# A second Strassen level for one product of seven, and what comes with it, in a four-layer graph-attention stack in fp32

## The chip, the cores and the metric

The kernel runs on one core of a Trainium2 chip. The metric is the device time of one execution in microseconds. Everything is fp32.

## The reference

The input `x` is 128 graphs of 64 nodes of 512 features, 8192 rows in all; `adj` is one 64 x 64 mask for all of them. Four layers follow one another, each `x = x + f(relu(layernorm(x)), adj)`:

```
layer 0: q, k, v = h@W + b;  softmax(q k^T / 8 + mask) v         8 heads of 64, no output product
layer 1: the same, then @ Wo + bo
layer 2: q = h Wq^T, k = h Wk^T, v = h Wv^T
         rel = adj^T * (q k^T);  rel / norm(rel, rows);  rel v   one head of 512
layer 3: qkv = h @ w_qkv;  masked softmax, as above;  o = (...) @ w_proj + b_proj
         f = o + layernorm(o) * gamma + beta
```

## The kernel before

**Tiling.** The rows are cut into 16 blocks of 512 tokens (`NB` = 16, `T` = 512), eight graphs each; a step `n` of the main loop is one block of one layer, 64 steps in all. A block's activations lie in SBUF as `hT`, features on partitions, so that TensorE can contract over them. Layer 2's q and k are folded into one matrix `a2` = Wq^T Wk ahead of time, so it has two projections (`g` and `v`); layer 0 has three (q, k, v), layers 1 and 3 four (q, k, v, o).

**Projections by Strassen.** A projection is a 512 x 512 by 512 x 512 product. It is done by Strassen's method with seven products of 256 x 256 by 256 x 256 in place of eight (`projection`, with `prod_T` for transposed and `prod_N` for plain results). The sums on the activations' side are `sums_x` (into `S` for `hT`, into `SO` for the attention's output `oT`, on POOL), those on the weights' side `sums_w`. Each of the seven products is four matmuls 256 columns wide into one PSUM bank. `ORDER` says in which order they run; two products that are added up share a bank (`X`). After each, ACT or DVE takes the bank out: product 1 to `s1`, 6 and 7 plus `s1` to `u2` and `u3`, 5 to `z5`, and the four corners Y11 (product 2), Y12 (3), Y21 (4, plus `u3`) and Y22 (`u3` + `z5`, on POOL) go where the `emit_...` function in use says.

**Attention.** `attend` runs in pieces between the projections: scores on TensorE (64 x 64 tiles, four at a time), mask and row maximum on DVE, subtraction on POOL, exponential on ACT, sum on DVE, scaling on POOL, and a transpose. `turn` is that transpose, used for `hT` too: DVE splits the fp32 words into two planes of 16 bits (`z`), SP issues a DMA transpose into `hp`, ACT joins the planes again. Then the products with v follow (`finish0` in layer 0, `finish13` in layers 1 and 3).

**Residual.** `load_xo` loads the block's input into `xo`; POOL adds a row of biases to it in layers 0, 1 and 3. In layer 3, `tail3` does the second layernorm: statistics of `o` on DVE, `xo += o` on POOL in four pieces, and two DVE instructions for each of the four tiles, the second one into `xo`. The tile `o` lies in `kT`'s buffer.

**Order of work.** All instructions are first recorded in `Plan`, in the order of the program, with the data that they read and write. `Plan.order` then schedules them as a list: for each engine, the ready step with the lowest rank comes next, by costs and latencies from `duration`; steps that read PSUM are moved up by `RUSH`. The result is a fixed order for each engine, issued as it stands. All instructions therefore carry the line of `record`, L193, in the profile, and are told apart by their tiles. Between the products of a projection, `tick` lets the waiting pieces of work (layernorm, attention, loads) record their next part.

**Buffers.** PSUM has eight banks: a ring of four for projections (`ps_mm`) and two double banks for attention (`ps_so`). In SBUF, `z` is a ring of four, `hp` of three, `s` (scores) of four, `xo` of two, and `qT`, `kT`, `v`, `oT`, `SO` are single.

```
ORDER = (1, 6, 5, 2, 7, 3, 4)
X = {1: 1, 2: 1, 6: 6, 7: 6, 5: 5, 3: 5, 4: 4}
```

Of the kernel before, what the change touches and what calls it, by code (L numbers as in the profile page):

```python
# [43 lines left out]
ORDER = (1, 6, 5, 2, 7, 3, 4)  # L44
ORDER0 = (1, 2, 5, 6, 3, 7, 4)
# [10 lines left out]
class Plan:  # L56
# [4 lines left out]
    def __init__(self, nc):  # L61
        self.nc = nc
        self.steps, self.products = [], []
        self.wrote, self.readers, self.known = {}, {}, {}
        self.group = None
        for e in ("tensor", "vector", "scalar", "gpsimd", "sync"):
            setattr(self, e, Engine(self, e))
# [48 lines left out]
    def add(self, eng, calls, reads, writes, busy, late):  # L116
# [12 lines left out]
        self.steps.append((eng, calls, deps, busy, late))  # L129

    def order(self):
        n = len(self.steps)
        wait = [len(s[2]) for s in self.steps]
        users = [[] for _ in range(n)]
        for i, s in enumerate(self.steps):
            for d in s[2]:
                users[d].append(i)

        rank = [i - RUSH * any(v.tensor.name.startswith("mm_") for c in s[1] for v in c[1][1:] if isinstance(v, bass.AP)) for i, s in enumerate(self.steps)]
# [10 lines left out]
        while len(out) < n:  # L150
# [17 lines left out]
            eng, _, _, busy, late = self.steps[i]  # L168
            if e == "sync":
                moved = max(moved, at + 1400) + late / 180  # L170
                late = moved + 600 - at - busy
            elif e == "vector" and late == PORT:
                busy += max(0.0, free["gpsimd"] - at)
                port = at + busy
            elif e == "gpsimd":
                busy += max(0.0, port - at)
            free[e] = at + busy
            out.append((at, i))
            for u in users[i]:
                same = self.steps[u][0] == e  # L180
                ready[u] = max(ready[u], at + busy + (0.0 if same and e != "sync" else late))
# [36 lines left out]

PORT = 150.5
RUSH = 60  # L220
# [4 lines left out]
def duration(eng, op, aps, a, k):  # L225
# [3 lines left out]
    if eng == "tensor":  # L229
# [3 lines left out]
        pass_ = max(n, P if m > HD else HD) * 0.842  # L233
# [17 lines left out]
    if eng == "gpsimd":  # L251
        if n <= HD:
            return (1010 if ALU.pow in a else 310), 120
        return n * (1.82 if n > D else 2.41), 120
    size = (2 if out.dtype == U16 else 4) * n * out.partition_size()
    return 1270 if k.get("transpose") else 520, size
# [3 lines left out]
def gnn_stack_kernel(  # L260
# [17 lines left out]
    def pool(name, bufs, **kw):  # L278
        return Ring(ctx.enter_context(tc.tile_pool(name=name, bufs=1, **kw)), bufs)

    const, wp, p1, p2, p4, p8, p3 = (
        pool("const", 1), pool("w", 4), pool("p1", 1), pool("p2", 2), pool("p4", 4), pool("p8", 8), pool("p3", 3),
    )
    rows = pool("rows", 3)
    sm = pool("sm", 4)
    dram = ctx.enter_context(tc.tile_pool(name="dram", bufs=1, space=bass.MemoryType.DRAM))
    ps_mm = pool("ps_mm", 4, space=bass.MemoryType.PSUM)
    ps_so = pool("ps_so", 2, space=bass.MemoryType.PSUM)
# [10 lines left out]
    pw = ps_mm.tile([P, KC, P], F32, tag="mm", name="pw")  # L299
# [3 lines left out]
    def dma(dst, src):  # L303
        plan.sync.dma_start(dst, src)

# [36 lines left out]
    def load_w(name, src):  # L342

        w = wp.tile([P, 7, 2, H2], F32, tag="w", name=name)


        def part(i, j):
            return src[i * H2 : (i + 1) * H2, j * H2 : (j + 1) * H2].rearrange("(c p) f -> p c f", p=P)

        dma(w[:, W11], part(0, 0))  # L350
        dma(w[:, W21], part(1, 0))
        dma(w[:, WT3], part(0, 1))
        dma(w[:, W22], part(1, 1))
        return w

    def sums_w(w, eng):
        tt = eng.tensor_tensor
        tt(w[:, WT1], w[:, WT3], w[:, W11], ALU.subtract)
        tt(w[:, WT2], w[:, W22], w[:, WT1], ALU.subtract)
        yield 1  # L360
# [3 lines left out]
    W = {}  # L364

    def weight(name, src, eng=gps):
        W[name] = load_w(name, src)
        yield 4
        yield from sums_w(W[name], eng)

# [4 lines left out]
    first = [load_w("q0", wq0)]  # L375
# [4 lines left out]
    first += [load_w("k0", wk0)]  # L380
# [16 lines left out]
    def raw(tag, src, nm):  # L397
        t = p1.tile([P, KC, D], F32, tag=tag, name=nm)
        for c in range(KC):
            dma(t[:, c, :], src[c * P : (c + 1) * P, :])  # L400
            yield 3
        return t

    def fold():
# [4 lines left out]
        for dc in range(KC):  # L409
            pa = ps_mm.tile([P, D], F32, tag="mm", name=f"pfa_{dc}")  # L410
# [4 lines left out]
            f = p4.tile([P, D], F32, tag="z", name=f"fa_{dc}")  # L415
            act.copy(f, pa)
            yield 1
# [4 lines left out]
        for ec in range(KC):  # L422
            f = p4.tile([P, KC, P], F32, tag="z", name=f"ft_{ec}")
            turn(f, rv[:, ec, :], f"v2_{ec}")
            yield 1
            dma(v2d.rearrange("(c p) e -> p c e", p=P)[:, :, ts(ec, P)], f)
            yield 1
# [17 lines left out]
    hTs, Ss, vs = {}, {}, {}  # L445
    ready = set()

    def turn(dst, src, nm):


        zp = p4.tile([P, D], F32, tag="z", name=f"zp_{nm}").bitcast(U16).rearrange("p (w f) -> p w f", w=2)
        dve.tensor_copy(zp, src.bitcast(U16).rearrange("p (f w) -> p w f", w=2))
        hp = p3.tile([P, 2, KC, P], U16, tag="hp", name=f"hp_{nm}")
# [5 lines left out]
    def layer_norm(n):  # L459
# [19 lines left out]
        if n == 0:  # L479
            for t in range(NT):  # L480
                z = xins[n][t]
                act.activation(z, z, AF.Relu, bias=nb[:, t : t + 1], scale=rs[:, t : t + 1])
                pt = ps_mm.tile([P, KC, P], F32, tag="mm", name=f"pz_{n}_{t}")
# [4 lines left out]
                if t == 1:  # L488
                    for i in range(WARM // 2):
                        pe.transpose(pw[:, i % KC, :], xins[n][0][:, ts(i % KC, P)], ident)  # L490
                (dve.tensor_copy if t else act.copy)(hT[:, :, ts(t, P)], pt)
        for t in range(NT) if n else ():
# [8 lines left out]
    def sums_x(tag, src, nm, eng):  # L501
# [7 lines left out]
        return {1: x11, 2: x12, 3: S[:, 3], 4: x22, 5: S[:, 0], 6: S[:, 1], 7: S[:, 2]}  # L509
# [19 lines left out]

    def projection(prod, w, xop, nm, emit, order=ORDER):  # L530

# [3 lines left out]
        def bank(i):  # L535
            banks[i] = ps_mm.tile([P, D], F32, tag="mm", name=f"pp{i}_{nm}")
# [6 lines left out]
        X = {1: 1, 2: 1, 6: 6, 7: 6, 5: 5, 3: 5, 4: 4}  # L543
        for i in order:
# [4 lines left out]
            prod(ps, w[:, BLOCKS[i]], xop()[i], first)  # L549
# [16 lines left out]
            elif i == 3:  # L566
                emit("Y12", ps, tmp["u2"])
            if i != order[-1]:
# [4 lines left out]
    def emit_plain(region):  # L573

        def emit(what, a, b=None):
# [15 lines left out]
    def emit_bias(region, bias):  # L591

        def emit(what, a, b=None):
# [37 lines left out]
    def scores(qT, kT, g, nm):  # L631

        pss = ps_so.tile([P, 2, 2, KC, G], F32, tag="so", name=f"pss_{nm}")
        for p in range(2):
            for c in range(KC):
                for h, x in QUARTERS:
                    b = h ^ x
                    at = ts(4 * g + 2 * p + b, G)  # L640
                    pe.matmul(
                        pss[half(x), b, p, c, :], qT[half(h), c, at], kT[half(h), c, at], start=True, stop=True
                    )
        return pss

    def attend(n, qT, kT, v, done):

        l = n // NB
        plan.begin()
        psss = [scores(qT, kT, g, f"{n}_{g}") for g in range(2)]  # L650
        plan.end(300)
        ss = [p4.tile([P, 2 * KC, 2, G], F32, tag="s", name=f"s_{n}_{g}") for g in range(2)]
        yield 1
        for s, pss in zip(ss, psss):
            for b in range(2):
                dve.tensor_tensor(
                    s[:, :, b, :], pss[:, b].rearrange("p q c j -> p (q c) j"),
                    MASKS[l].unsqueeze(1).to_broadcast([P, 2 * KC, G]), ALU.add,
                )
            sf = s.rearrange("p q b j -> p (q b) j")  # L660
# [3 lines left out]
            yield 2  # L664
        yield 1
        for s in ss:
# [6 lines left out]
            yield 2  # L673
        yield 1

        aTs = []
        for s in ss:
            aT = s.rearrange("p (q c) b j -> p q c (b j)", q=2)
            aTs.append(aT)
            for p in range(2):  # L680
                if n < N - 1:
                    turn(aT[:, p], s[:, p * KC : (p + 1) * KC].rearrange("p c b j -> p (c b j)"), f"a_{n}_{p}")
                else:
                    pt = ps_mm.tile([P, KC, P], F32, tag="mm", name=f"pa_{n}_{p}")
# [4 lines left out]
                    act.copy(aT[:, p], pt)  # L689
                yield 1  # L690
        yield 1
        yield from done(aTs, v)
# [25 lines left out]
    def load_xo(n):  # L718
# [5 lines left out]
        if l in xo_row:  # L724
            row = R[xo_row[l]]
            for t in range(NT):
                gps.tensor_tensor(xos[n][:, t, :], xos[n][:, t, :], row, ALU.add)
                if t < NT - 1:
                    yield 1
        ready.add(("xo", n))  # L730

    def finish0(n):
        def done(aTs, v):


            assert ("xo", n) in ready and ("v", n) in ready
            plan.begin()
            pos = []
            for g, aT in enumerate(aTs):
                po = ps_so.tile([P, 2, 2, H2], F32, tag="so", name=f"po_{n}_{g}")  # L740
                pos.append(po)
                for p in range(2):
                    for c2 in range(2):
                        for h in range(2):
                            for b, y in QUARTERS:
                                j = b ^ y
                                f = c2 * P + h * HD
                                pe.matmul(
                                    po[half(y), j, p, f : f + HD], aT[half(b), p, 2 * j + c2, half(h ^ b)],
                                    v[half(b), 2 * g + p, j * H2 + f : j * H2 + f + HD], start=True, stop=True,  # L750
                                )
            plan.end(300)
            yield 1
            for g, po in enumerate(pos):
                for j in range(2):
                    xv = xos[n][:, 2 * g : 2 * g + 2, j * H2 : (j + 1) * H2]
                    dve.tensor_tensor(xv, po[:, j], xv, ALU.add)
            yield 1
            store(n, xos[n])
        return done  # L760
# [3 lines left out]
    def finish13(n):  # L764
        def done(aTs, v):

            assert ("v", n) in ready
            oTs[n] = p1.tile([P, KC, T], F32, tag="oT", name=f"oT_{n}")
            plan.begin()
            pos = []  # L770
            for g, aT in enumerate(aTs):
                po = ps_so.tile([P, 2, 2, KC, G], F32, tag="so", name=f"po_{n}_{g}")
                pos.append(po)
                for p in range(2):
                    for c in range(KC):
                        for b, h in QUARTERS:
                            f = c * P + h * HD
# [347 lines left out]
```

## Time and profile before

| What | us |
|---|---|
| median of 3 runs | 2843.88 (2843.86 to 2844.54) |
| the profiled execution, its own time | 2844.57 |
| its span, first to last instruction | 2842.8 |
| TensorE busy | 2828.4 |
| VectorE (DVE) busy | 2037.6 |
| GpSimd (POOL) busy | 1840.5 |
| ScalarE (ACT) busy | 1248.0 |

PE stands for TensorE's matmuls and PEld for its weight loads, which run beside them. Granted clock of TensorE in the profiled execution: 0.999. A group of instructions reads as engine, operation, result<-operands by tile names, shape, count, then busy time in us, mean ns of one, and the idle time ahead of them with what ended it. Busy time of matmuls counts overlapping records once; a record is longer than the distance to the next. SP issues all DMAs; the 16 DMA engines were busy for half of the span (50.0%).

### The profile page before, as it was taken

Reading aid. Unit: us, or ns where it says so; the run is one execution under the profiler, and the core shown is the slowest. Engines: PE = TensorE matmul, PEld = TensorE weight load, DVE = VectorE, ACT = ScalarE, POOL = GpSimd, SP = SyncE. Lnnn points to the kernel's source line nnn. Section 1 sums busy time; section 2 is a strip of 40 time slices with the busy share of each in tenths; the row PEclk is TensorE's granted clock in tenths of the full one; section 3 lists DMA queues with packets and bytes.
Section 4 is the critical chain, followed back from the end, with each engine's and each line's share of the span. In section 5 each row is a group of like instructions: output and inputs, shape, how many; then the busy total and the mean of one; then the engine's idle time right before and its main releaser. Section 6 shows DMA issues by size and latency. Waiting matters only on the chain.

```text
span 2842.8 us, 62036 instructions
## 1 busy us (share of the span) xinstructions
PE 2828.4 (99%) x25833; PEld 2471.6 (87%) x25833; DVE 2037.6 (72%) x3104; ACT 1248.0 (44%) x1589; POOL 1840.5 (65%) x1349
## 2 busy tenths in 40 slices
PE   9999999999999999999999999999999999999998
PEld 8878888888888888888888888888888888888887
DVE  7767778876767767667666555555688888778787
ACT  4555555454443534534434343443444444444442
POOL 6555566656766667667677334344678687787796
PEclk9999999999999999999999999999999999999999
DMA  6766666556453533533546565756433433433432
GB/s 158 163 137 156 143 146 134 127 128 163 105 120 80 124 95 82 131 85 86 136 114 156 136 162 143 164 128 157 120 86 94 119 86 95 112 91 96 109 84 66
DMA packets 634890, 342.29 MB, mean 120 GB/s; under 512 B 485232, under 2 KB 566384, under 8 KB 634608
## 3 DMA queue, kind: packets, MB, share of 16 engines
q1 hardware_dynamic: 634608, 338.32, 50.0%
q8 instruction: 202, 3.31, 0.5%
q14 instruction: 80, 0.66, 0.1%
HBM read 152.61 MB, written 69.21 MB: 78 GB/s over the span
## 4 chain that ended last, share of the span: by engine, by line
PE 96%; DVE 3%; issue 0%; POOL 0%; DMA 0%; ACT 0%; POOLq 0%; SPq 0%; DVEq 0%
PE mm L193 88%; PE so L193 8%; DVE z L193 1%; DVE st L193 0%; POOL s L193 0%; DVE u L193 0%; DVE sr L193 0%; DVE kT L193 0%; DMA xin<-in_x_dram 0%; DVE mv L193 0%; DVE w L193 0%; DVE xo L193 0%; ACT xin L193 0%; ACT oT L193 0%; POOLq L1120 0%
## 5 line engine op out<-in xcount | busy, mean ns | idle before, releaser
L193 PE MATMUL mm<-S,w 128*128 128x256 f32 x3584 | 817.2, 380 | 0.0
L193 PEld LDWEIGHTS mm<-S,w 128*128 128x128 f32 x3584 | 679.3, 190 | 93.8 <-issue 1.0
L193 PE MATMUL mm<-hT,w 128*128 128x256 f32 x2688 | 629.9, 380 | 4.0 <-DVE kT L193 3.7
L193 DVE TENSOR_TENSOR u<-mm,s 128x512 f32<-128x512 f32 x414 | 284.9, 688 | 480.1 <-PE mm L193 342.3
L193 PEld LDWEIGHTS mm<-hT,w 128*128 128x128 f32 x2688 | 509.6, 190 | 75.5 <-DVE kT L193 5.3
L193 PE MATMUL mm<-w,S 128*128 128x256 f32 x2048 | 472.8, 381 | 0.0
L193 PEld LDWEIGHTS mm<-w,S 128*128 128x128 f32 x2048 | 385.5, 190 | 53.8 <-issue 0.5
L193 ACT COPY hT<-hp 128x1024 uint16<-128x1024 uint16 x252 | 332.7, 1350 | 90.3 <-DMA hp<-z 90.2
L193 PE MATMUL mm<-w,hT 128*128 128x256 f32 x1536 | 366.4, 381 | 0.0
L193 ACT COPY s<-hp 128x1024 uint16<-128x1024 uint16 x188 | 252.3, 1352 | 204.3 <-DMA hp<-z 197.1
L193 ACT COPY s<-mm 128x512 f32<-128x512 f32 x211 | 123.0, 583 | 490.0 <-PE mm L193 419.0
L193 POOL TENSOR_TENSOR s<-s,mx 128x1024 f32<-128x1024 f32 x96 | 183.3, 1911 | 226.9 <-DVE mx L193 224.9
L193 PEld LDWEIGHTS mm<-w,hT 128*128 128x128 f32 x1536 | 289.2, 190 | 40.2 <-DVE v L193 0.2
L193 POOL TENSOR_TENSOR xo<-xo,row 128x512 f32<-128x512 f32 x192 | 286.1, 1510 | 8.4 <-DMA xo<-in_x_dram 5.7
L193 DVE COPY z<-s 128x1024 uint16<-128x1024 uint16 x188 | 278.2, 1501 | 6.7 <-POOL s L193 6.6
L193 DVE COPY z<-xin 128x1024 uint16<-128x1024 uint16 x252 | 245.3, 988 | 37.6 <-ACT xin L193 34.0
L193 ACT ACTIVATE xin<-xin,nb,rs 128x512 f32<-128x512 f32 x256 | 195.4, 808 | 90.5 <-DVE nb L193 89.9
L193 PE MATMUL mm<-w,SO 128*128 128x256 f32 x992 | 224.3, 379 | 0.0
L193 POOL TENSOR_TENSOR qT<-u,z 128x512 f32<-128x512 f32 x64 | 87.5, 1367 | 202.2 <-DVE u L193 189.8
L193 PEld LDWEIGHTS mm<-w,SO 128*128 128x128 f32 x992 | 188.5, 190 | 25.6
L193 POOL TENSOR_TENSOR s<-s,sr 128x1024 f32<-128x1024 f32 x96 | 187.3, 1963 | 34.2 <-DVE sr L193 32.1
L193 ACT ACTIVATE s<-s 128x1024 f32<-128x1024 f32 (+1 forms) x112 | 108.1, 966 | 200.3 <-POOL s L193 144.3
(98 smaller groups left out, 3667.7 us busy)
## 6 DMA issues: line engine op xcount, KB each, us to landing
xin<-x SPq DMA_DIRECT2D x192, 256.0 KB, 4.0
xo<-x SPq DMA_DIRECT2D x64, 512.0 KB, 4.5
xin<-in_x_dram SPq DMA_DIRECT2D x64, 256.0 KB, 3.2
x<-xo SPq DMA_DIRECT2D x64, 256.0 KB, 2.5
x<-xo SPq DMA_DIRECT2D x128, 128.0 KB, 2.5
x<-xo SPq DMA_DIRECT2D x32, 512.0 KB, 3.0
out_dram<-xo SPq DMA_DIRECT2D x30, 512.0 KB, 3.0
xo<-in_x_dram SPq DMA_DIRECT2D x32, 256.0 KB, 3.2
```

The source lines that it names most:

```text
L193: getattr(getattr(self.nc, eng), op)(*a, **k)
```

## The change

1. **A second level for product 4.** In the weights of `LEVEL2` (layer 1's and 3's q, k, v, o; layer 2's a2 and v2) product 4 is itself done by Strassen's method: seven products of quarters, one matmul each, 128 columns wide. It runs in two parts, "4a" (four of them) after product 5 and "4b" (three) at the end (`FINER`). `close_2` puts the corner Y21 together, from the bank, `u3` and a new small tile `q`: two copies on ACT, two additions on DVE, three on POOL, and two on DVE in place of one. `sums_x` and `sums_w` get four small sums each; on the activations' side they overwrite a quarter of `hT` or `oT` that is no longer needed (in layer 2 another buffer, as `hT` is).
2. **Accumulating transfers.** In layer 3 the row of biases, and `o` in `tail3`, are added to `xo` by a DMA with `accum_op`, issued by POOL, in place of four POOL additions each.
3. **Alike banks.** All eight PSUM banks stand in one `Pool`, taken and given back by name. Scores and values take four single banks, and are recorded as two steps which `join` keeps together on TensorE. The values are recorded after the next step's first projection (`values`), the scores right after k (`begin_scores`).
4. **Rings.** `z` has six tiles (four before), `hp` five (three), `s` two (four).
5. **Plan.** `RUSH` is 100 (60), `duration` has a floor of 111 ns for a pass with more than 64 weight columns and costs for the new transfers; the preliminary loads of weights are spread out.

The diff, cut to its core:

```diff
 ORDER = (1, 6, 5, 2, 7, 3, 4)
+FINER = (1, 6, 5, "4a", 2, 7, 3, "4b")
...
-RUSH = 60
+LEVEL2 = {c + l for l in "13" for c in "qkvo"} | {"a2", "v2"}
+RUSH = 100
...
-        pass_ = max(n, P if m > HD else HD) * 0.842
+        pass_ = max(n * 0.842, 111 if m > HD else HD * 0.842)
...
+    if "accum_op" in k:
+        return 1100, 2000 + size / 150
...
+    zs, hps = pool("zs", 6), pool("hps", 5)
-    ps_mm = pool("ps_mm", 4, space=bass.MemoryType.PSUM)
-    ps_so = pool("ps_so", 2, space=bass.MemoryType.PSUM)
+    mm = Pool([mm.tile([P, D], F32, tag=f"mm_{i}", name=f"mm_{i}") for i in range(8)])
...
+    def add(dst, src):
+        gps.dma_start(dst, src, accum_op=ALU.add)
...
 sums_w
+        t, e = w[:, WT4], W2[name]
+        if finer(name):
+            tt(e[:, 0], t[:, 0, P:], t[:, 0, :P], ALU.subtract)
+            tt(e[:, 1], t[:, 1, P:], e[:, 0], ALU.subtract)
+            yield 2
+            tt(e[:, 2], t[:, 1, :P], e[:, 1], ALU.subtract)
+            tt(t[:, 0, P:], t[:, 1, P:], t[:, 0, P:], ALU.subtract)
...
 sums_x
+        a, b, c, d = [x22[:, j, ts(i, P)] for i in range(2) for j in range(2)]
+        F = fine or [x21[:, j, ts(i, P)] for i in range(2) for j in range(2)]
+        if needs2:
+            tt(F[0], c, d, ALU.add)
+            tt(F[1], F[0], a, ALU.subtract)
+            tt(F[2], a, c, ALU.subtract)
+            tt(F[3], b, F[1], ALU.subtract)
...
+    def prod_2(prod, ps, name, xop, todo):
+        w = W[name][:, WT4]
+        e = W2[name]
+        ws = {1: w[:, 0, :P], 2: w[:, 1, :P], 3: w[:, 1, P:], 4: e[:, 2], 5: e[:, 0], 6: e[:, 1], 7: w[:, 0, P:]}
+        at = {1: (0, 0), 2: (0, 0), 5: (0, 1), 3: (0, 1), 6: (1, 1), 7: (1, 1), 4: (1, 0)}
+        for i in todo:
+            x, out = xop["quarters"][i], quarter(ps, prod, *at[i])
+            a, b = (ws[i], x) if prod is prod_T else (x, ws[i])
+            pe.matmul(out, a, b, start=i == 1, stop=True, skip_group_check=True)
+
+    def close_2(prod, ps, q, base, dst, bias):
+        u2, u3, z5 = q[:, 1], q[:, 2], q[:, 3]
+        y12 = quarter(base, prod, 0, 1)
+        gps.tensor_tensor(y12, y12, u2, ALU.add)
+        y2 = base[:, :, P:] if prod is prod_T else base[:, 1, :].rearrange("p (v f) -> p v f", v=2)
+        gps.tensor_tensor(y2, y2, u3.unsqueeze(1).to_broadcast([P, 2, P]), ALU.add)
+        gps.tensor_tensor(dst[:, 1, P:], base[:, 1, P:], z5, ALU.add)
+        for at in ((slice(None), 0, slice(None)), (slice(None), 1, slice(0, P))):
+            if bias is None:
+                dve.tensor_tensor(dst[at], ps[at], base[at], ALU.add)
+            else:
+                dve.scalar_tensor_tensor(dst[at], ps[at], bias[at[1]], base[at], ALU.add, ALU.add)
...
 projection
+            if i in BLOCKS:
+                prod(ps, w[:, BLOCKS[i]], xop()[i], first)
+            else:
+                pv = ps.rearrange("p (u v) -> p u v", u=2)
+                prod_2(prod, pv, name, xop(), (1, 5, 6, 4) if i == "4a" else (2, 7, 3))
...
+            elif i == "4a":
+                q = p1.tile([P, 4, P], F32, tag="q", name=f"q_{nm}")
+                act.copy(q[:, 0], quarter(pv, prod, 0, 0))
+                dst, base, bias = emit("close")
+                if bias is None:
+                    act.copy(q[:, 3], quarter(pv, prod, 0, 1))
...
+                dve.tensor_tensor(q[:, 1], quarter(pv, prod, 1, 1), q[:, 0], ALU.add)
+            elif i == "4b":
+                dve.tensor_tensor(q[:, 2], quarter(pv, prod, 1, 1), q[:, 0], ALU.add)
...
+                close_2(prod, pv, q, base, dst, bias)
...
 attend
+    def begin_scores(n, qT, kT):
+        first = len(plan.steps)
+        psss = scores(qT, kT, n)
+        plan.join(first, 300)
+        spawn(attend(n, take_scores(n, psss)))
...
 load_xo
+            if l < 3:
...
+            else:
+                add(xos[n], row.unsqueeze(1).to_broadcast([P, NT, D]))
...
 tail3
-            gps.tensor_tensor(xo[:, t, :], xo[:, t, :], o[:, t, :], ALU.add)
+            if t == NT - 1:
+                add(xo, o)
...
 main loop, layers 0, 1 and 3
             run(projection(prod_T, f"q{l}", ...
+            values()
             run(projection(prod_T, f"k{l}", ...
+            begin_scores(n, qT, kT)
             run(projection(prod_N, f"v{l}", ...
-            spawn(attend(n, qT, kT, v, done), 3 if n < N - 1 else 0)
```

## The prediction

> **What bounds the kernel now.** I read the page first: the busy shares, then the chain that ended last, then the costliest groups.
>
> ```profile
> span 2842.8 us, 62036 instructions
> ...
> PE 2828.4 (99%) x25833; PEld 2471.6 (87%) x25833; DVE 2037.6 (72%) x3104; ACT 1248.0 (44%) x1589; POOL 1840.5 (65%) x1349
> ...
> PE 96%; DVE 3%; issue 0%; POOL 0%; DMA 0%; ACT 0%; POOLq 0%; SPq 0%; DVEq 0%
> ...
> L193 PE MATMUL mm<-S,w 128*128 128x256 f32 x3584 | 817.2, 380 | 0.0
> L193 PEld LDWEIGHTS mm<-S,w 128*128 128x128 f32 x3584 | 679.3, 190 | 93.8 <-issue 1.0
> ```
>
> TensorE is busy for 99% and makes up 96% of the chain; its largest group never sat idle. A matmul's record lasts 380 ns, but matmuls overlap, so the price of one is the distance between starts. The timeline of TensorE in layer 1 shows it:
>
> ```profile
> 1031.76 1.89 PE L193 MATMUL mm<-hT,w 128*128 128x256 f32 x8
> 1033.48 3.62 PE L193 MATMUL mm<-S,w 128*128 128x256 f32 x16
> ```
>
> One Strassen product is eight passes (four fp32 matmuls, each recorded as two) and the next begins 1.72 us later: (1.89 - 0.38) / 7 = 0.216 us a pass, 1.726 us a product. The page's six groups 256 columns wide hold 11,656 passes, so 2515 us of the span is this work. Time can leave in bulk only there.
>
> The busy time by stretch, from the middles of layers 1 and 3 (columns: PE, PEld, DVE, ACT, POOL, each with its count):
>
> ```profile
> 750.00:1500.00 750.00, 749.39 (x6886) 657.52 (x6885) 516.08 (x748) 314.98 (x409) 516.86 (x372) 1.00 0.43 104
> 2050.00:2750.00 700.00, 696.29 (x6401) 609.72 (x6400) 569.53 (x799) 298.76 (x366) 548.06 (x394) 1.00 0.40 97
> ```
>
> Score blocks follow one another every 52.8 us in layer 1 and 53.4 us in layer 3. Per block of 512 tokens that is POOL 36.4 and DVE 36.3 us in layer 1, POOL 41.8 and DVE 43.4 us in layer 3. These are the engines that the change loads.
>
> **What the skill says.** The Trainium skill, "TensorE: Matmul & The Clock Gate", section "LDWEIGHTS (loading the stationary operand)", prices a weight load by its columns, columns / 1.2 ns: 107 ns for 128. The trace agrees: at the end of a score block, eight loads take 1.59 us,
>
> ```profile
> 1012.66 1.59 PEld L193 LDWEIGHTS mm<-w,hT 128*128 128x128 f32 x8
> ```
>
> and with six gaps of 0.216 and a last record of 0.190 this leaves 0.10 for the first gap[...]. "SBUF — State Buffer", section "Who interferes with whom", says that VectorE's two-port copies, and its instructions with two SBUF inputs, exclude POOL's reads. The trace agrees: the copy z<-s takes 1501 ns beside POOL's work, the same shape z<-xin 988.
>
> **The change, part by part.**
>
> *TensorE.* In ten weights (a2, v2, and q, k, v, o of layers 1 and 3) product 4 becomes seven products of quarters: 14 passes 128 columns wide in place of 8 passes of 256. Projections concerned: layer 1, 64; layer 2, 32; layer 3, 48 + 15 (the last o is done without Strassen); 159. A fp32 pass 128 wide with ordinary operands isn't in the trace. Its nearest rows are the four-piece transposes near the end, 128 wide with a load for each:
>
> ```profile
> 2810.97 0.60 PE L193 MATMUL mm<-ident,s 128*128 128x128 f32 x4
> ...
> L193 PE MATMUL mm<-ident,s x16: 272/273/329, 2811.0 to 2816.4; 128*128 128x128 f32 x16
> ```
>
> (0.60 - 0.273) / 3 = 0.109 us from start to start. The floor is half of 0.216, 0.108; I take 0.110, because load (0.108) and stream are then equally long and nothing is left to hide a slip. Product 4 then costs 14 x 0.110 = 1.540, a gain of 0.186 us, times 159 = **29.6 us** (0.109: 31.8; 0.111, which the changed cost table itself assumes: 27.4). The gain is zero at 0.1233 us a pass. If no load were hidden, a pass would be 0.108 + 0.108 and the part would lose 159 x (3.02 - 1.73) = 206 us.
>
> *The joints of product 4* (close_2, and two copies and two additions into the tile q). POOL gets three small additions for each projection, 128, 256 and 128 wide, and four of 128 for each set S and SO that needs them. POOL's 512-wide addition in quiet takes 1266 ns. In proportion, 128 and 256 columns are 0.32 and 0.63 us; with the skill's 4497 ns at 2048 columns ("GPSIMD Engine Reference", section "3.1 Elementwise — side-by-side cycle accounting") the slope is 2.10 ns and they are an estimated 0.46 and 0.73. I take 0.39 and 0.68. Layers 1 and 3 have four projections and two sets each: 4 x 1.46 + 8 x 0.39 = 9.0 us a block (7.6 to 10.3). DVE loses one 512-wide addition (0.68) and gets one of 256 (0.425, the row s<-mm,adj) and three of 128 (0.30 each, on the line through those two): +0.64 for each projection, +2.6 us a block. ACT gets two copies of 128, about 0.33 each on the line from 583 ns (512) and 417 (256): +2.6 us. The finer weight sums are forty additions in all, some 16 us of POOL over the whole kernel, done ahead of need.
>
> *Layer 3's transfers.* Eight POOL additions a block go:
>
> ```profile
> L193 POOL TENSOR_TENSOR xo<-xo,row 128x512 f32<-128x512 f32 x52 | 79.6, 1556 | 0.0
> L193 POOL TENSOR_TENSOR xo<-xo,kT 128x512 f32<-128x512 f32 x52 | 75.4, 1479 | 0.0
> ```
>
> 4 x 1.556 + 4 x 1.479 = 12.1 us. In come two accumulating DMAs of 1 MB issued by POOL, of which the trace shows none. The skill ("DMA: Bandwidth & Descriptors", section "Anatomy of one DMA — SWDGE (gpsimd) path") gives 2.0 us + bytes / 436,000 for a plain one: an estimated 4.4 us; with the destination read as well, twice the bytes, 6.8. From this trace's 512 KB loads at 4.5 us the same reasoning gives 9 for 1 MB and 18 if the bytes count double. I take 8, range 4.4 to 18, and an estimated 1 us of POOL for each issue (0 to 3).
>
> *Sums per block.* Layer 1: POOL 36.4 + 9.0 = 45.4 of 52.1 us (87%), DVE 38.9. Layer 3: POOL 41.8 - 12.1 + 9.0 + 2 = 40.7 of 52.7, DVE 46.0 (87%), ACT 25. Layer 2 had POOL at 126.4 of 330 us and gets about 4.5 a block of 28.7. All stay under TensorE. A load as tight was already carried: in layer 3, POOL's 41.8 us and the DVE instructions that exclude it (eight copies, at their shortest 0.68 us, and eight with two SBUF inputs at 0.73: 11.3 us) leave nothing of 53.4 us, even if part of POOL's time is itself waiting, and TensorE was still busy for 696 of 700.
>
> *What I cost at nothing.* All eight PSUM banks in one pool: projections hold four as before, scores and values four as before. The value products move behind the next q: from the end of scores at 1012.5 to values at 1040.5 the softmax now has 28 us; behind v, o and q it has three projections, 36 us. In layer 0 only v and q lie between, 24 us, for a chain of 28; there k's products, ready and independent, go first. Longer rings for z and hp let SP's transposes (3.3 us to landing) wait less; SP gets no new issue. Were this cover gone, each block could stand for the 2 us that scores or values take.
>
> New waits: scores wait for k's last corner, which now passes DVE, three POOL additions and DVE again, some 3 us instead of 1.4; v's seven products are ready meanwhile. I put 3 us in all for slips (-4 to 20). **Sum:** 2842.8 - 29.6 + 3 = 2816.2 us of span; the profiled execution took 2844.6, the median of the runs is 2843.9, so 2843.9 - 26.6 = **2817 us**.
>
> **The rivals.**
> *(a) Half is given back, 2836 us.* With POOL at 87% in layer 1, the small additions at 0.46 us and 5.5 us of DVE's copies that lock it out make it late for S, SO and the corners, and TensorE waits: 0.6 us, half a 512-wide addition, in each of 32 blocks, 19 us. For: 9 us more on POOL. Against: layer 3 carried as much with 4 us of idle TensorE in 700.
> *(b) Slower, 2875 us: the accumulating transfer comes late.* Place: tail3 of layer 3. DVE's first xo<-z,rs,xo waits for the whole transfer, and behind it in DVE's queue stand the next products' evictions out of PSUM, for which TensorE's next banks wait; the projection's free banks last about two products, 4 us. With the cost table's 10 us from issue to landing as the plan, a landing at 14 is free, and each us beyond costs 15 us (15 blocks). It decides at 16 us, where the 30 us are gone; at 18 it gives 2843.9 - 29.6 + 60 = 2875. For: the 18 us bound. Against: the DMA engines are only 0.40 busy there.
> *(c) The change does not do what it says.* Fp32 loads are exposed at 128 columns: at 0.123 us a pass nothing moves, at 0.135 it is 159 x 14 x 0.0117 = 26 us slower, at worst 3050. For: ordinary loads last 190 ns in the records, the transposes' 140. Against: the 0.108 between two loads.
> *(d) POOL falls behind its plan,* which prices the small additions at 0.31 us, in every block: 20 x 0.15 = 3 us of lag, and with half of it never caught up 32 blocks x 1.5 = 48 us: 2843.9 - 29.6 + 3 + 48 = 2865. Against: POOL idles 16 us a block in layer 1, where it can catch up.
>
> **How the numbers follow.** Forecast 0.66 (2808 to 2831), (a) 0.13, (b) 0.10, (c) 0.06, (d) 0.05. About 0.2%, 5.7 us, is what a measurement of this kernel can tell from no change. Faster: the forecast and 0.08 of (a), 0.74. Same: the rest of (a) and 0.02 of (c), 0.07. Slower: 0.19. The range of 2804 to 2850 reaches down to the floor price (31.8) with 8 us of waits gained, and up over (a); it leaves out (b), (d) and most of (c).
>
> **What would show it.** Right: 2226 matmuls 128 wide with starts 0.108 to 0.111 apart, TensorE still at 99%, layer 1's score blocks 0.75 us closer, layer 3's too, layer 0's unchanged. Wrong: starts at 0.12 or more; DVE idle before xo<-z,rs,xo; TensorE idle behind POOL in layer 1; an accumulating transfer over 14 us.

## The result and the profile after

The changed kernel takes 2832.59 us (median of 5 runs, 2831.8 to 2833.34) against 2844.22 before: a ratio of 0.9959, interval 0.9944 to 0.9973. It is 11.6 us faster, where 26.6 were forecast. Its profiled execution took 2832.0 us, its span is 2829.9. The page after:

```profile
span 2829.9 us, 65896 instructions
...
PE 2803.2 (99%) x26787; PEld 2481.2 (88%) x26787; DVE 1999.9 (71%) x3549; ACT 1318.5 (47%) x1907; POOL 2138.8 (76%) x2089
...
PE 93%; POOL 3%; DMA 1%; DVE 1%; issue 1%; ACT 0%; POOLq 0%; SPq 0%; ACTq 0%; DVEq 0%
...
L217 PE MATMUL mm<-S,w 128*128 128x256 f32 x3584 | 812.0, 379 | 1.9 <-ACT z L217 1.9
```

TensorE is still busy for 99%, but POOL now holds 3% of the chain, 85 us, where it had less than one per cent. POOL went from 1840.5 to 2138.8 us. The stretches in the middle of layers 1 and 3 (PE, PEld, DVE, ACT, POOL):

```profile
750.00:1500.00 750.00, 750.00 (x7279) 670.64 (x7278) 525.03 (x897) 345.97 (x529) 658.66 (x658) 1.00 0.42 106
2050.00:2750.00 700.00, 698.84 (x6778) 624.67 (x6777) 546.53 (x974) 323.72 (x475) 589.82 (x589) 1.00 0.63 137
```

There TensorE hardly waits. The timeline of TensorE in layer 1 gives the price of the quarters and the new distance of the blocks:

```profile
1108.92 0.83 PE L217 MATMUL mm<-hT,w 128*128 128x128 f32 x6
...
1118.31 2.10 PE L217 MATMUL mm<-kT,qT 64*64 64x64 f32 x128
```

Six passes with a last record of 0.275 are (0.83 - 0.275) / 5 = 0.111 us apart; over all neighbouring pairs of ordinary 128-wide passes the median distance of starts is 0.112. Score blocks follow one another every 52.1 us, from 52.8: 0.65 us for four projections, 0.163 for each, which is 0.112 a pass again. In layer 3 the distance is 52.1 us too, from 53.4 on average. So the steady blocks gained nearly what they should. What is missing was lost between the layers and at the end. The same view of the 93 us ahead of layer 2, before and then after:

```profile
1472.00:1565.00 93.00, 93.00 (x755) 81.58 (x757) 55.96 (x85) 36.51 (x46) 76.08 (x59) 1.00 0.61 158
```

```profile
1472.00:1565.00 93.00, 87.89 (x735) 77.08 (x734) 55.66 (x95) 32.38 (x50) 89.17 (x98) 1.00 0.50 132
```

POOL is busy for 96% of the second one and TensorE idle for 5 us. POOL's longest group in the 95 us from 1470 is the sums of weights for the next layers. The kernel before had 16 of them there, all 512 wide; the changed one has 14 of these (18.7 us), and twelve small ones, 128 wide, besides (6.1 us):

```profile
L193 POOL TENSOR_TENSOR w<-w 128x512 f32<-128x512 f32 x16 | 20.6, 1300 | 0.6
```

```profile
L217 POOL TENSOR_TENSOR w<-w 128x512 f32<-128x512 f32 (+1 forms) x26 | 24.6, 962 | 0.5
```

The chain that ended last runs through POOL here, from 1513 to 1558 us, with no other engine in between. Its longest pieces up to 1540 us (start, length, what):

```profile
1514.55 2.13 POOL w L217 x3
...
1520.57 3.78 POOL w L217 x3
...
1530.68 3.74 POOL SO L217 x3
...
1536.19 2.45 POOL xo L217 x2
```

Count a start of a matmul as late when it comes over 0.35 us after its predecessor allowed it (0.216 us later for 256 columns, 0.112 for 128, some ns for the small tiles), and leave out the first 20 us. Then TensorE lost 3.8 us at the start of layer 1 (675 to 731 us), 6.0 from layer 1 to 2 (1513 to 1564), 3.1 at the start of layer 3 (2033 and 2053) and 1.6 near the end (2802), 14.5 in all. The kernel before had 5.6 us in all, of which 4.4 in layer 3. After TensorE's last matmul the kernel before ran on for 7.8 us, the changed one for 10.6. There DVE waits for a transfer:

```profile
DVE xo L217 <- DMA xo<-w: 5.6, 1, 5.6
```

### The profile page after: what moved, and what is told of

Its sections match the earlier page's. It is cut to its first block, busy times and chain, and to the rows that moved or that the text cites. A ratio compares the mean times of both kernels' runs of the same rounds, so it can differ in the third digit from the quotient of the medians.

```text
span 2829.9 us, 65896 instructions
## 1 busy us (share of the span) xinstructions
PE 2803.2 (99%) x26787; PEld 2481.2 (88%) x26787; DVE 1999.9 (71%) x3549; ACT 1318.5 (47%) x1907; POOL 2138.8 (76%) x2089
## 4 chain that ended last, share of the span: by engine, by line
PE 93%; POOL 3%; DMA 1%; DVE 1%; issue 1%; ACT 0%; POOLq 0%; SPq 0%; ACTq 0%; DVEq 0%
PE mm L217 93%; DMA hp<-z 1%; POOL S L217 1%; POOL w L217 1%; DMA xo<-w 0%; POOL s L217 0%; POOL xo L217 0%; POOL SO L217 0%; POOL u L217 0%; DVE xo L217 0%; DVE z L217 0%; DMA xin<-in_x_dram 0%; DVE st L217 0%; ACT s L217 0%; DVE w L217 0%
## 5 line engine op out<-in xcount | busy, mean ns | idle before, releaser
L217 PE MATMUL mm<-hT,w 128*128 128x256 f32 (+1 forms) x3040 | 612.2, 347 | 2.9 <-ACT q L217 1.9
L217 PE MATMUL mm<-w,hT 128*128 128x256 f32 (+1 forms) x1696 | 349.2, 347 | 0.7 <-ACT s L217 0.7
L217 DVE COPY z<-s 128x1024 uint16<-128x1024 uint16 x188 | 225.0, 1218 | 64.7 <-POOL s L217 64.6
L217 POOL TENSOR_TENSOR xo<-xo,row 128x512 f32<-128x512 f32 x128 | 169.1, 1340 | 66.2 <-DMA xo<-in_x_dram 66.2
L217 POOL TENSOR_TENSOR u<-u,q 128x128 f32<-128x128 f32 (+1 forms) x256 | 175.3, 693 | 30.4 <-DVE q L217 22.7
```

The costliest lines, as they stand in the source:

```text
L217: getattr(getattr(self.nc, eng), op)(*a, **k)
```

## The experiments

All ratios are to the kernel before, which took 2844.2 to 2844.4 us beside each of them. "The changed kernel" is the 2832.6 us above. The interval of a ratio reaches some 0.0007 to 0.0014, 2 to 4 us, to each side. A smaller difference between two of these kernels is firm only where a trace shows where it comes from.

**1. The level alone taken away.**

```diff
-LEVEL2 = {c + l for l in "13" for c in "qkvo"} | {"a2", "v2"}
+LEVEL2 = set()
```

> The changed kernel with product 4 undivided in all weights (LEVEL2 empty); all else as changed. Theory (the level itself saves 159 x 0.158 = 25 us at the measured 0.112 us a pass, and pays about 10 us of it back in TensorE waits at the layer boundaries, where POOL has its pieces on top of the weight sums; the rest of the change is worth little): the boundary waits go with the pieces, TensorE gets 25 us back, so 2832.6 + 25 - 10 = 2847, give or take 4, and under 6 us of TensorE waits over 0.35 us outside the start. Rival (the order of work, the pool of banks or the paused weight loads make the boundary waits, whatever product 4 is): the waits stay and the time is 2856 to 2859. Rival (the level pays in full and the rest costs it): 2832.6 + 25 = 2858 as well, but with the 15 us of waits seen at other places than the boundaries.

Measured: 2848.19 us, ratio 1.0017 (1.0008 to 1.0027). The waits at the start of layer 1 and from layer 1 to 2 were gone, and 1.1 us were left at the start of layer 3. So the new order alone doesn't make them, the level does; experiment 4 shows by which part. But the runs spread from 2843.9 to 2859.9, and the profiled one, the slowest (span 2858.1), has a single wait of 13 us in layer 3:

```profile
ACT s L217 <- DMA hp<-z: 14.6, 2, 13.9
...
PE mm L217 <- ACT z L217: 12.7, 1, 12.7
```

ACT waits for a transpose, with two accumulating transfers of 1 MB issued at 2170.2 and 2181.7 us beside it, and TensorE waits for ACT. The chain shows the transpose, issued together with the second transfer; that one took 19.6 us:

```profile
2181.71 17.73 DMA hp<-z
```

From 2100 to 2780 us a transpose takes a median of 5.0 us from issue to landing here (at most 10.7 of those with a landing on record, to which this one doesn't belong); 3.4 and 5.7 in the changed kernel.

**2. The level and the transfers taken away**, so that order, banks, rings and spread loads are left; with the edit of experiment 1:

```diff
-            if l < 3:
+            if l < 4:
                 for t in range(NT):
...
-            if t == NT - 1:
-                add(xo, o)
+            gps.tensor_tensor(xo[:, t, :], xo[:, t, :], o[:, t, :], ALU.add)
```

> Product 4 undivided and layer 3's additions on POOL: of the change only the order of work, the alike banks, the rings and the spread loads are left. Theory (these are worth only the waits that the kernel before had in layer 3, 0.6 us a block): 2838 to 2842, blocks of layer 3 at 52.8 us where they were 53.4 on average, and runs within 1 us of each other, since no accumulating transfer meets a transpose. Rival (the order itself costs): 2846 or more, like the undivided run with transfers (2843.9 to 2859.9).

Measured: 2839.13 us, ratio 0.9982 (0.9975 to 0.9989), 17 runs within 2 us; transposes at a median of 3.1 us. The rest of the change is worth 5.2 us by itself. It takes away the 4.4 us of waits in the old layer 3, whose blocks now follow one another every 52.8 us. How the 5.2 us divide among order, banks and rings wasn't tried.

**3. The transfers alone taken away**, with the edit just shown and the level kept.

> Layer 3's additions to xo are done by POOL again, in four pieces each, in place of the accumulating transfers; all else as changed. Theory: POOL's 43.9 us a block become about 43.9 + 12.1 - 2.7 = 53.3 us of a block of 52.1, so POOL sets the pace of layer 3: blocks 1 to 3 us longer, 15 to 45 us in all, 2845 to 2875. Rival (POOL has room since part of its busy time is waiting for DVE's lock): within 4 us of 2832.6, and the end of the kernel 3 us shorter since no transfer of 13.5 us is waited for there: 2829.

Measured: 2900.47 us, ratio 1.0193 (1.018 to 1.0207): 68 us slower than the changed kernel, more than the theory gave. Layer 3 from 2100 us:

```profile
2100.00:2800.00 700.00, 660.22 (x6264) 584.12 (x6264) 560.56 (x898) 305.61 (x445) 655.71 (x618) 0.98 0.38 94
```

POOL at 94% sets the pace and TensorE idles for 40 of 700 us. Without the transfers the level doesn't pay in layer 3. Level and transfers can't be judged one at a time: 2839.1 us with neither, 2848.2 with the transfers alone, 2900.5 with the level alone, 2832.6 with both.

**4. Weight sums off POOL.** Four kernels: all sums of weights loaded after the start on DVE; those of layers 2 and 3 alone; the small sums of the finer level alone; the last two together.

```diff
-        spawn(weight(name, SRC[name]))
+        spawn(weight(name, SRC[name], dve))
```

> The sums on the weights' side go from POOL to DVE for every weight loaded after the start (some 88 small and large additions, 24.6 us of POOL in the stretch from layer 1 to 2). Theory (POOL is full at the boundaries): POOL's busy share in the 92 us ahead of layer 2 falls from about 98% to about 70%, the TensorE waits there (7 to 8 us between 1472 and 1565 us) and near 726 us shrink to under 3 us, and the time falls by 6 to 10 us, to 2823 to 2827. Rival (weights come late, by their paused loads, or values and scores in the new order make the waits): no change beyond 2 us. Rival (DVE becomes what is late): slower by up to 10 us, with TensorE waiting on DVE at the same places.

```diff
+        spawn(weight(name, SRC[name], gps if name[1] == "1" else dve))
```

> The weight sums of layers 2 and 3 go to DVE, those of layer 1 stay on POOL. Theory (POOL is full only from layer 1 to 2; in layer 1's start DVE has no room, which is why moving those sums gave some of the gain back): the waits between 1472 and 1565 us go (8 us), those of the sums-on-DVE run at 776, 812 and 863 us don't come, and the time is 2823 to 2826. Rival (the place of the waits is a matter of the fixed order alone and moves with any change): 2827 to 2833 with as many waits elsewhere.

```diff
         if finer(name):
+            tt = dve.tensor_tensor
             tt(e[:, 0], t[:, 0, P:], t[:, 0, :P], ALU.subtract)
```

> Only the forty small additions of the finer weight sums go to DVE (21 us of POOL in the whole kernel, some 7 us of them between 1472 and 1565 us); the large ones stay on POOL. Theory (POOL is over its capacity there by about the 5 us that TensorE waits): the waits shrink from 7 to 8 us to 1 to 4, 2826 to 2830. Rival (what matters is the chain of the large sums, not POOL's load): no change within 1.5 us.

> All small weight sums on DVE, and the large ones too for layers 2 and 3. Theory: both parts relieve the same stretch, so the gains of 7 us don't add up; what is left are the waits at layer 1's start (3 to 5 us), layer 3's start and the end: 2823 to 2826. Rival (they add up): 2818 to 2820.

Measured: 2826.91 (ratio 0.994, 0.9927 to 0.9952), 2825.57 (0.9934, 0.9922 to 0.9946), 2825.49 (0.9934, 0.9922 to 0.9947) and 2826.62 us (0.9937, 0.9924 to 0.995). The stretch ahead of layer 2 with the small sums alone moved:

```profile
1472.00:1565.00 93.00, 93.00 (x860) 83.05 (x859) 63.67 (x114) 36.89 (x56) 89.94 (x92) 1.00 0.57 141
```

TensorE waits no more, with POOL as busy as ever: it was over its capacity by a few us, and taking the twelve small additions in this stretch (12 x 0.52 = 6.1 us) off it was enough. Moving the large sums as well, which leaves POOL at 74 to 75 of 93 us, adds nothing. Each edit makes a new order of all instructions, so the cure might be the order's luck; the other runs speak against that. The five kernels of experiments 3, 6, 7 and 8 keep the level and the small sums on POOL, and TensorE has 5.7 to 6.0 us of late starts in this stretch in each. The seven of experiments 4 and 9 have the small sums of layers 2 and 3 off POOL, and none has a late start there. All four keep 4.5 to 5.0 us of late starts at the beginning of layer 1 (675 to 863 us), where the changed kernel has 3.8.

**5. The level in layer 3 alone.**

```diff
+LEVEL2 = {c + l for l in "3" for c in "qkvo"}
```

> The second level in layer 3's four weights alone (63 projections). Theory: TensorE saves 63 x 0.158 = 10 us there, layers 1 and 2 lose their 96 x 0.158 = 15 us and with them the waits of 8 us from layer 1 to 2 and 4 us at layer 1's start: 2832.6 + 15.2 - 11 = 2837, with PE at 93 of 93 us ahead of layer 2. Rival (the waits from layer 1 to 2 come from layer 3's weights, q3 and k3, whose sums run there too): waits of 4 us or more stay, 2841.

Measured: 2835.39 us, ratio 0.9969 (0.9957 to 0.9981), TensorE at 93.00 of 93 us ahead of layer 2. The 96 projections of layers 1 and 2, worth 15 us at 0.158, bring only 2.8 us net in the changed kernel (its runs, 2831.8 to 2833.3, and these, 2834.5 to 2835.9, don't overlap).

**6. Loads of a weight all at once.**

```diff
-        yield from load_w(name, src, 3)
+        now(load_w(name, src))
+        yield 4
```

> The four quarters of a weight are loaded at once, four ticks ahead of its sums, as in the kernel before, in place of three ticks between them. Theory (POOL's load is what is short at the boundary, not the weights' arrival): within 2 us of 2832.6, with waits between 1472 and 1565 us still 5 us or more. Rival (weights that come late make the waits): the waits there fall under 2 us and the time to 2825.

Measured: 2837.79 us, ratio 0.9977 (0.9968 to 0.9986): 5 us slower, with 8.0 us of late starts at the beginning of layer 1 in place of 3.8. From layer 1 to 2 there are still 5.7 us, with the weights loaded earlier, so late weights are not the cause there; both expectations missed that the spread loads help.

**7. What sets the pass.**

```diff
+            m = 120 if i in (2, 7, 3) else P
-            pe.matmul(out, a, b, start=i == 1, stop=True, skip_group_check=True)
+            pe.matmul(out[:, :m], a, b[:, :m], start=i == 1, stop=True, skip_group_check=True)
```

> The three quarter products of part 4b stream 120 columns in place of 128 (the last eight columns of those quarters are left out of the sums); 4a keeps 128; loads and all else as changed. If the weight load sets the 0.112 us of a pass, 4b's passes stay at 0.112 and the time at 2832.6. If the stream sets it, 4b's passes fall to about 0.105[...], 159 x 6 x 0.007 = 6.7 us less, 2826.

Measured: 2832.38 us. Six passes of part 4b:

```profile
1108.69 0.82 PE L217 MATMUL mm<-hT,w 128*128 128x120 f32 x6
```

0.82 in place of 0.83 us, and a median distance of 0.112 for both widths: less to stream doesn't make the pass shorter. That rules the stream out and fits the weight load, which was left as it was; a load of another width, which would show it, wasn't run.

**8. The end.** The last o on POOL, then the last row of biases on POOL instead.

```diff
+            if n == N - 2:
+                gps.tensor_tensor(xo[:, t, :], xo[:, t, :], o[:, t, :], ALU.add)
-            if t == NT - 1:
+            elif t == NT - 1:
                 add(xo, o)
```

> Only the last tail3 (block 62) adds o to xo on POOL in four pieces; the fourteen before it keep the accumulating transfer. Theory (DVE's queue at the end of the kernel stands behind the transfer of 13.5 us, from 2796.5 to 2810.0): the end comes 3 us earlier, 2829.6, with the distance from TensorE's last matmul to the end of the span back from about 10.6 to about 7.7 us. Rival (the end is set by the last block's own chain): no change, within 1 us.

```diff
-            if l < 3:
+            if l < 3 or n == N - 1:
```

> Only the last block's row of biases is added on POOL, so that the accumulating transfer of o for block 62, issued 0.9 us after it, has the DMA engines to itself. Theory (two accumulating transfers of 1 MB at once make the second one take 13.5 us, DVE waits 5.6 us for it at 2804 to 2810 and the last four evictions stand behind it): the transfer lands in 8 to 10 us and the time falls by 2 to 4 us, to 2829 to 2831. Rival (POOL's four pieces delay the last softmax as the last pieces of o did when put on POOL): 2833 to 2835.

Measured: 2834.34 us (0.9967, 0.9955 to 0.998), a miss: the part after TensorE's last matmul fell from 10.6 to 8.9 us, but POOL's four pieces (5.4 us from 2795.5) stand ahead of its additions for the last v, for which TensorE waited 3.5 us in place of 1.6 (the softmax had its scaling on POOL before that); and 2828.44 us (0.9945, 0.9932 to 0.9958). In the second the transfer of the last o, now alone, lands after 7.2 us, not 13.5, DVE's wait for it is gone, and the part after the last matmul is 7.9 us. That explains 2.7 of the 4.1 us.

**9. Remedies together.** The small sums on DVE and the last row on POOL; with these, layer 3's first row on POOL too; or, with these, the activations' sums of layer 1's first block on DVE (`dve if n in (0, NB) else gps`).

> The small weight sums on DVE and the last block's row on POOL, the two separate remedies together. Theory (they cure waits at different places, layer 1 to 2 and the end): the gains of 7.1 and 4.1 us add up, 2832.6 - 11.2 = 2821.4, give or take 1. Rival (the end is shared, since any change of the order moves it): 2824 to 2826.

> As the run before, and also layer 3's first row of biases on POOL. Theory (the first accumulating transfer, 13.2 us long, delays the transposes ahead of the first values of layer 3, where TensorE waits 1.8 and 1.4 us near 2033 and 2053): these two waits go, 2 to 3 us less than the run before. Rival (POOL is full there too): the same or slower.

> As the first run of this group, and also the first block of layer 1 has its activations' sums on DVE. Theory (POOL's load is what TensorE waits for at layer 1's start, 726 and 730 us): the 3 us of waits there shrink, 1 to 3 us less than the first run of this group. Rival (DVE's own load there, 92 of 120 us, or the order of the softmax makes them): the same or slower.

Measured: 2822.71 (0.9922, 0.9909 to 0.9936), 2823.72 (0.9926, 0.9913 to 0.9938) and 2828.71 us (0.9943, 0.993 to 0.9955). The two remedies nearly add up, 9.9 of 11.2 us: to the small sums on DVE the last row adds 2.8 us, just what the part after the last matmul loses. The first kernel is the fastest of all, 21.7 us under the one before. Of the waits near 2033 and 2053 us it has only the second left, 1.4 us. Without the first transfer of layer 3 that one goes too, and the few transposes there (five, and three in the first kernel) land in a median of 3.5 us, not 4.9, as the theory says; but waits of 1.2, 0.5 and 0.4 us come at 2225, 2170 and 2483 in the new order, so nothing is gained. Off POOL, the first block's sums cost 6 us: DVE, or the order, sets the start of layer 1. Which of the two stays open.

## Why the prediction was right or wrong

**TensorE's saving: right in kind, 4 us too large.** The 159 projections and 2226 passes are as counted; the pass is 0.112 us, not 0.110, so 159 x 14 x 0.002 = 4.5 us of the 29.6 don't exist. The transposes at 0.109 were a poor stand-in: their loads are shorter in the records (140 ns against 190), which the prediction noted under rival (c) and didn't price. The stream doesn't set the pass (experiment 7), which fits (c)'s exposed load, but the pass stays 0.011 us short of the break-even.

**The step that failed: the finer weight sums "done ahead of need", at nothing, and 3 us "for slips".** The span lost 11.8 us in that place, where 3 were taken: late starts rose from 5.6 to 14.5 us, and the part after TensorE's last matmul from 7.8 to 10.6. Both terms rested on the middles of layers. Between layers 1 and 2, POOL's spare 17 of 93 us had to take the pieces of every projection and twelve small weight sums, beside the large ones that were there before, and TensorE waited for 6.0 us. With the small sums on DVE that wait is gone and the kernel 7.1 us faster.

**POOL's sum: near in the middles, in part by luck.** Layer 1's block has 658.66 / 750 x 52.1 = 45.8 us of POOL, where 45.4 were forecast. But its small additions take 0.46 us in quiet, as the line through the longer ones said, not the 0.39 taken, and the pieces come to 10.5 us a block, not 9.0; POOL's other work fell from 36.4 to 35.2. Layer 3 has 43.9, not 40.7: an issue is 1.4 us, not 1, and u<-u,q takes 0.64 us for 128 columns and 0.96 for 256 there, 0.49 and 0.76 in layer 1. The "16 us a block" in which POOL was to catch up under (d) are those of the kernel before; with the pieces there were 6.7 by the prediction's own sum. DVE came out lower than forecast, 36.5 us a block in layer 1 (38.9) and 40.7 in layer 3 (46.0), since instructions of it got shorter, the copies z<-s from 1744 to 1328 ns in the one and from 1469 to 1117 in the other. None of this held TensorE up in the middles.

**The transfers.** The bias row lands in 8.1 us, the value taken; the transfer of o in 13.6 (median), close to the 14 that (b) called free. DVE then waits 44.2 us in 13 blocks with no wait of TensorE behind it. The 13.6 belong to the pair: the two are issued 0.9 us apart in each block but the first, and in that one, with 19 us between them, o lands in 7.6. (b)'s mechanism came once, at the end: 13.5 us, and DVE's queue stood 5.6 us behind it; parting the two transfers there gives 2.8 us (experiment 9) to 4.1 (experiment 8). What no term held is that transposes land later beside these transfers. "Layer 3's transfers" was also counted only as 12.1 us of room on POOL; experiment 3 shows that the level depends on them in layer 3 (68 us).

**What was costed at nothing and gained.** Order, banks, rings and loads brought 5.2 us.

**The sum as measured**, from the traces of the two kernels. Span before, 2842.8 us; less 25.1 for the level at 0.112; plus 8.9 for late starts (14.5 less 5.6, the gain of the new order in layer 3 included); plus 2.9 at the end: 2829.5, where 2829.9 were measured. Of the late starts, the 6.0 us from layer 1 to 2 are explained by experiment 4; those at the starts of layers 1 and 3 and the one near the end are counted, not explained. Rival (a), half given back through a late POOL, is nearest in time and cause, but its place was wrong: not 0.6 us in each block, but the passages between layers and the end. (d) is out: steady blocks run at 52.1 us.

## What to carry to other kernels

Read the spare time of the helper engines at the transitions, not only in the steady middle: work that is "done ahead" is done there, all at once. When matmuls are made narrower until load and stream are equal, take the price from a row with the same kind of load; 2% of a pass was 4.5 us here. An accumulating transfer takes additions off a full engine, but here the transposes that the next step waits for landed later beside it, and of two issued together the second landed in 13.6 us where one alone took 7.2.

## What the runs showed of the hardware

Ordinary fp32 passes of 128 columns with a load each start 0.112 us apart, and 120 columns don't change that (experiment 7). An accumulating transfer of 1 MB took 0.9 to 1.7 us of POOL to issue; it landed after 7.2 us at the quickest (the last o alone, experiment 8) and 19.6 at most (experiment 1). Of two issued 0.9 us apart the first landed in 8.1 us and the second in 13.6, so both were there 14.4 us after the first issue, about twice 7.2. DMA transposes had a median of 3.1 us without such transfers (experiment 2), 3.4 beside the pairs of the changed kernel, and 5.0 in the slowest run of experiment 1, where the two are issued 11.4 us apart.
